# One third of nine table loads is split into DMAs of 16, 35, 35, 21 and 21 rows

## The chip, the core and the metric

The kernel runs on one core of a Trainium2 chip. A core has five engines that run their own instruction streams: PE (TensorE, matrix products), DVE (VectorE), ACT (ScalarE), POOL (GpSimd) and SP (SyncE, here used only to issue DMAs). Sixteen DMA engines move data between HBM, the chip's large memory, and SBUF, the core's 128-partition working memory. PSUM is the small memory that PE writes into. The metric is the device time of one launch in microseconds (us); the median of ten runs is compared.

## The reference

For each of 1024 users the function gathers up to 50 item embeddings of length 128, forms running means over time, normalizes them over the batch, feeds them through a leaky integrate-and-fire step, and multiplies the mean spike count with the whole embedding table.

```python
emb = emb_table.at[0].set(0.0)              # 100001 x 128, float32
e = emb[seq]                                # seq: 1024 x 50
prefix = jnp.cumsum(e, axis=1)
denom = jnp.minimum(t_idx[None, :], lengths[:, None]).astype(e.dtype)
uF = prefix / denom[:, :, None]
y = (uF - uF.mean(axis=0)) * lax.rsqrt(uF.var(axis=0) + BN_EPS) * gamma + beta
def step(v, x):
    v = v + (x - v) / TAU
    spike = atan_spike(v - V_TH)            # 1 where v >= V_TH
    return (v - spike * V_TH, spike)
_, spikes = lax.scan(step, v0, moveaxis(y, 1, 0))
scores = spikes.mean(axis=0) @ emb.T        # 1024 x 100001, float32
```

The scores alone are 409.6 MB, and they must be written to HBM.

## The kernel before

**First stage.** The loop `for t in range(T)` gathers the 50 time steps with indirect DMAs on POOL, accumulates them in PSUM, and does the statistics and the spike step on DVE and ACT. It ends with the spike counts in `countA`, `countB` and `countC`, 128 users to a block of columns.

**Second stage.** The table is cut into 98 parts of 1024 rows (`HALF`); the last has 673. `WIDTHS` groups the parts into 21 column groups of the output: 4 of two parts, 4 of three, then 13 of six (the last a little narrower). For each column group `c` and each of the 8 blocks of users `n`, PE multiplies the counts with the split table parts (`product`, line 154 of the file), DVE and ACT take turns in copying the sums out of PSUM into an output tile `o` (lines 483 and 485), and SP stores that tile with one DMA (`store`, line 163). From the ninth group on such a store is 128 rows of 24 KB, 3 MB in all, and there are three output tiles in turn, so that the filling of one tile waits until the store of three before has landed.

**The loads.** A part of the table lies in SBUF as 128 partitions with 8 rows of 512 bytes each, 4 KB in one piece. `fetch(r, q, n)` loads `n` parts starting with part `q` into the row tile `r`. The first 38 parts (`held`) are loaded by SP during the first stage. The others are loaded by ACT in the second stage, three parts at a time (`GROUP // 2`), after the second and the fifth block of a column group (`n in (1, 4)`), so that there are two loads to a column group; two row tiles take turns. Such a load is one DMA of 1.5 MB (line 102) with 384 pieces of 4 KB. Later `prepare` transposes a part on PE, and ACT and DVE split it into a high and a low half.

```python
            if n in (1, 4) and c >= MIDDLE and to_fetch < parts:
                g, k = divmod(to_fetch - TWICE, GROUP)
                if k or to_split >= (g - 1) * GROUP + TWICE:
                    ...
                    fetch(r, to_fetch, GROUP // 2)
                    to_fetch += GROUP // 2
```

The last load is shorter: two whole parts (line 102), then the tail part in a DMA of five times 128 rows (line 111) and one of 33 rows (line 116).

**Order.** The kernel records its instructions in program order for each engine (`manual_schedule`). SP and ACT are in-order: a DMA that must wait holds up everything behind it on the same engine. Completion of the DMAs of SP and ACT is told by eight semaphores, used in turn (the trace names them 101 to 106, 117 and 118); a DMA is issued only when the one that had the same semaphore eight DMAs earlier has landed.

Of the kernel before, what the change touches and what calls it, by code (L numbers as in the profile page):

```python
# [20 lines left out]
P = 128  # L21
BN_EPS = 1e-5
V_TH = 1.0
HALF = 1024
KQ = HALF // P
BANK = 512
GROUP = 6
# [3 lines left out]

WIDTHS = 4 * [2] + 4 * [3] + 13 * [6]
NARROW, MIDDLE = 4, 8


@with_exitstack
def rec_kernel(
# [38 lines left out]
    held = AHEAD * GROUP + TWICE  # L76
# [8 lines left out]
    def size(q):  # L85
        return min(HALF, N - q * HALF)

    def group(g):
        at = g if g < AHEAD else AHEAD - 2 + g % 2
        r = rowp.tile([P, GROUP, HALF], F32, tag=f"rows{at}", name=f"rows_{g}")  # L90
        for k in range(GROUP):
            rows[g * GROUP + (TWICE if g else 0) + k] = r[:, k, :]
        return r

    def fetch(r, q, n):

        engine = nc.sync if q < held else nc.scalar
        k = q if q < GROUP else (q - TWICE) % GROUP
        n = min(n, parts - q)
        whole = n - (size(q + n - 1) < HALF)  # L100
        if whole:
            engine.dma_start(
                out=r[:, k : k + whole, :],
                in_=table[q * HALF : (q + whole) * HALF, :].rearrange("(q p k) d -> p q (k d)", p=P, k=KQ),
            )
        if whole < n:
            full, rest = divmod(size(parts - 1), P)
            c1 = (parts - 1) * HALF
            r = r[:, k + whole, :].rearrange("p (k d) -> p k d", d=D)
            if full:  # L110
                engine.dma_start(
                    out=r[:, :full, :],
                    in_=table[c1 : c1 + full * P, :].rearrange("(k p) d -> p k d", p=P),
                )
            if rest:
                engine.dma_start(out=r[:rest, full, :], in_=table[c1 + full * P : N, :])
# [49 lines left out]
    with ExitStack() as ph:  # L166
# [16 lines left out]
        nc.sync.dma_start(out=gb[:, 1:2], in_=beta.rearrange("(d o) -> d o", o=1))  # L183
        first = group(0)
        fetch(first, 0, GROUP)
        for g in range(1, AHEAD):
            fetch(group(g), g * GROUP + TWICE, GROUP)
# [91 lines left out]
        def over(t, v):  # L279

            d = lp.tile([P, B], BF16, tag="d", name=f"d_{t}")
            nc.scalar.activation(d, v, AF.Identity, bias=less)  # L282
            return d
# [7 lines left out]
        whole = slice(0, B)  # L291
# [6 lines left out]
        for t in range(T):  # L298
# [33 lines left out]
            r = sp.tile([P, 1], F32, tag="r", name=f"r_{t}")  # L332
# [14 lines left out]
            q = sp.tile([P, 1], F32, tag="q", name=f"q_{t}")  # L347
# [20 lines left out]
            if not last:  # L368
# [6 lines left out]
                d = over(t, v)  # L375
# [3 lines left out]
                if t in (T - 8, T - 6):  # L379
                    q = (t - T + 8) // 2  # L380
                    pair(q)
                    prepare(q, vp.tile([P, HALF], F32, tag="v1", name=f"pt_{q}"))
                    if q == TWICE - 1:
                        for k in range(TWICE):
                            rows[GROUP + k] = first[:, k, :]
                        nc.sync.dma_start(
                            out=first[:, :TWICE, :],
                            in_=table[GROUP * HALF : (GROUP + TWICE) * HALF, :].rearrange(
                                "(q p k) d -> p q (k d)", p=P, k=KQ
                            ),  # L390
# [48 lines left out]
    for c, W in enumerate(WIDTHS):  # L439
# [30 lines left out]
        for n in range(NB):  # L470
# [26 lines left out]
# [3 lines that stand above are left out]
                    if k == 0:  # L500
                        r = group(g)
                    fetch(r, to_fetch, GROUP // 2)
                    to_fetch += GROUP // 2
# [21 lines left out]
```

## Time and profile before

| What | Value |
|---|---|
| Median of 10 runs | 1579.63 us (1578.96 to 1580.17) |
| The profiled execution's own time | 1579.85 us |
| Its span, first to last instruction | 1577.7 us |
| Mean granted clock of TensorE | 0.941 |
| Bytes from HBM, to HBM | 77.69 MB, 409.60 MB |
| Busy share of the span: PE, DVE, ACT, POOL | 72%, 60%, 42%, 25% |
| First load of the second stage is issued | 782.2 us |
| Last load of the second stage is issued | 1416.6 us |

The span leaves out some 2.2 us around the instructions (1579.85 less 1577.7). The busy shares are means over two stages with different limits: the first stage ends at about 520 us and hardly uses the DMA engines after its start, the second uses them all the time.

### The profile page before, as it was taken

How to read it: one execution, taken by the hardware profiler on the slowest of the kernel's cores; microseconds unless marked ns; L12 is line 12 of the kernel's file. 1: busy time of each engine (PE TensorE's matmuls, PEld its weight loads, DVE VectorE, ACT ScalarE, POOL GpSimd, SP SyncE). 2: the span in 40 equal slices, each digit the busy share in tenths (PEclk: the TensorE clock that was granted, in tenths of full speed). 3: DMA queues.
4: the chain of work that ended last, by engine and by line, in shares of the span. 5: the costliest groups of instructions: out<-in, count | busy, mean ns of one | idle time of the engine just before them, and what ended most of it. 6: DMA issues, size and time to landing. Idle time of an engine off the chain costs nothing.

```text
span 1577.7 us, 12239 instructions
## 1 busy us (share of the span) xinstructions
PE 1128.8 (72%) x4450; PEld 801.4 (51%) x4450; DVE 945.0 (60%) x1125; ACT 668.2 (42%) x697; POOL 387.9 (25%) x408
## 2 busy tenths in 40 slices
PE   4544444444445988889887888888888787888884
PEld 2211111111122766668666666666666676666663
DVE  5777777767777665567555545545555545545552
ACT  2333333333333554555444444444444444444542
POOL 7777777777777000000000000000000000000000
PEclk9999999999975999999999999999999989999997
DMA  9611111111121899999999999999999999999998
GB/s 350 233 52 53 52 54 52 52 53 52 53 79 47 345 416 403 422 419 402 421 431 429 430 428 427 417 422 428 417 414 417 423 428 423 414 416 425 406 429 340
DMA packets 51897, 488.12 MB, mean 309 GB/s; under 512 B 10075, under 2 KB 11004, under 8 KB 30588
## 3 DMA queue, kind: packets, MB, share of 16 engines
q1 hardware_dynamic: 30464, 429.81, 64.8%
q0 software_dynamic: 12800, 26.24, 5.7%
q10 hardware_dynamic: 8572, 31.28, 5.0%
q8 instruction: 35, 0.57, 0.1%
q14 instruction: 26, 0.21, 0.0%
HBM read 77.69 MB, written 409.60 MB: 309 GB/s over the span
## 4 chain that ended last, share of the span: by engine, by line
DMA 52%; POOL 18%; PE 12%; issue 8%; ACT 5%; DVE 2%; another core or an unknown queue 0%; ACTq 0%; SPq 0%; POOLq 0%; DVEq 0%
DMA scores<-o 45%; POOL e L196 18%; PE po L154 11%; DMA e<-in_L_rec_emb_table,idx 5%; ACT o L485 5%; DMA rows<-in_L_rec_emb_table 2%; DVE o L483 1%; PE pt L124 0%; ACT pairs L146 0%; PE pre L309 0%; DVE pairs L147 0%; DMA idx<-in_r_seq 0%; DVE uF L318 0%; ACTq L485 0%
## 5 line engine op out<-in xcount | busy, mean ns | idle before, releaser
L483 DVE TENSOR_SCALAR o<-po 128x1024 f32<-128x1024 f32 x391 | 464.4, 1221 | 345.6 <-DMA scores<-o 304.2
L485 ACT ACTIVATE o<-po 128x1024 f32<-128x1024 f32 (+1 forms) x391 | 389.2, 1018 | 541.5 <-DMA scores<-o 319.8
L196 POOL DMA_INDIRECT e<-in_L_rec_emb_table,idx x400 | 382.3, 956 | 123.7 <-issue 112.4
L154 PE MATMUL po<-pairs,countB 128*128 128x512 f32 x1136 | 303.5, 413 | 63.3 <-ACT o L485 46.4
L309 PE MATMUL pre<-ident,e 128*128 128x128 f32 x400 | 180.8, 464 | 231.7 <-DMA e<-in_L_rec_emb_table,idx 231.3
L154 PEld LDWEIGHTS po<-pairs,countB 128*128 128x128 f32 x1136 | 217.6, 197 | 125.5 <-ACT o L485 61.1
L154 PE MATMUL po<-pairs,countC 128*128 128x512 f32 x852 | 236.4, 424 | 50.5 <-ACT o L485 50.4
L309 PEld LDWEIGHTS pre<-ident,e 128*128 128x128 f32 x400 | 73.3, 184 | 342.0 <-DMA e<-in_L_rec_emb_table,idx 341.2
L154 PEld LDWEIGHTS po<-pairs,countC 128*128 128x128 f32 x852 | 166.8, 202 | 96.5 <-ACT o L485 62.1
L147 DVE TENSOR_TENSOR pairs<-pt,pairs 128x1024 fp32r<-128x1024 f32 x71 | 86.2, 1222 | 95.6 <-ACT pairs L146 95.4
L318 DVE SCALAR_TENSOR_TENSOR uF<-rlen,pre 128x512 f32<-128x512 f32 x100 | 68.3, 683 | 112.7 <-PE pre L309 112.6
L124 PE MATMUL pt<-ident,rows 128*128 128x128 f32 x782 | 112.9, 292 | 9.0 <-issue 4.9
L124 PEld LDWEIGHTS pt<-ident,rows 128*128 128x128 f32 x782 | 102.1, 153 | 27.4 <-issue 12.9
L333 ACT ACTIVATE r<-mv,eps 128x1 f32<-128x1 f32 x50 | 14.8, 295 | 226.4 <-DVE mv L329 226.4
L154 PE MATMUL po<-hi,countB 128*128 128x512 f32 x216 | 88.2, 408 | 17.6 <-ACT o L485 12.7
L270 PE MATMUL pre<-zT,ls 128*128 128x512 f32 x100 | 77.5, 777 | 23.0 <-DVE uF L318 19.1
L154 PE MATMUL po<-lo,countB 128*128 128x512 f32 x216 | 85.4, 397 | 0.0
L282 ACT ACTIVATE d<-v,less 128x1024 bf16<-128x1024 f32 x49 | 54.5, 1113 | 63.5 <-DVE v L366 63.5
L154 PE MATMUL po<-hi,countC 128*128 128x512 f32 (+1 forms) x162 | 68.8, 425 | 14.7 <-ACT o L485 14.7
L146 ACT CAST pairs<-pt 128x1024 fp32r<-128x1024 f32 x71 | 71.8, 1012 | 15.3 <-PE pt L124 15.1
L154 PE MATMUL po<-pairs,countA 128*128 128x512 f32 x284 | 71.0, 394 | 6.7 <-ACT o L485 6.7
L363 ACT ACTIVATE v<-uF,hgb,a 128x1024 f32<-128x1024 f32 x49 | 59.2, 1208 | 30.5 <-DVE a L359 30.5
(78 smaller groups left out, 824.6 us busy)
## 6 DMA issues: line engine op xcount, KB each, us to landing
scores<-o SPq DMA_DIRECT2D x96, 3072.0 KB, 20.2
scores<-o SPq DMA_DIRECT2D x32, 1536.0 KB, 8.9
scores<-o SPq DMA_DIRECT2D x30, 1024.0 KB, 8.6
rows<-in_L_rec_emb_table ACTq DMA_DIRECT2D x19, 1536.0 KB, 29.1
scores<-o SPq DMA_DIRECT2D x8, 2896.5 KB, 17.3
rows<-in_L_rec_emb_table SPq DMA_DIRECT2D x6, 3072.0 KB, 27.8
e<-in_L_rec_emb_table,idx POOLq DMA_INDIRECT x400, 2.5
rows<-in_L_rec_emb_table SPq DMA_DIRECT2D x1, 1024.0 KB, 4.8
```

Source lines behind the costliest of these rows:

```text
L124: nc.tensor.transpose(pt[:, k0 : k0 + kw], r[:kw, k0 : k0 + D], ident[:kw, :kw])
L146: nc.scalar.copy(vh, vp)
L147: nc.vector.tensor_tensor(vl, vp, vh.bitcast(F32), ALU.subtract)
L154: nc.tensor.matmul(po[:, :kw], lhsT=counts[n], rhs=part[:, k0 : k0 + kw], start=j == 0, stop=j == 1,)
L196: nc.gpsimd.indirect_dma_start(out=es[t][:, n * P : (n + 1) * P], out_offset=None, in_=table, in_offset=bass.IndirectOffsetOnAxis(ap=idx[: ...
L270: nc.tensor.matmul(pre[h], lhsT=l, rhs=zT[:, h * BANK : (h + 1) * BANK], start=t == 0, stop=False, skip_group_check=True,)
L282: nc.scalar.activation(d, v, AF.Identity, bias=less)
L309: nc.tensor.matmul(pre[h][:, k : k + P], lhsT=e[:, h * BANK + k : h * BANK + k + P], rhs=ident, start=False, stop=last, is_transpose=True, ...
L318: nc.vector.scalar_tensor_tensor(uF[:, cs], rlen[:, cs], 1.0 / (t + 1), pre[h], ALU.max, ALU.mult)
L363: nc.scalar.activation(vt, uF[:, cs], AF.Identity, bias=hgb[:, 1:2], scale=a)
L483: nc.vector.tensor_scalar_mul(o[:, h0 : h0 + hw], po[:, :hw], 1.0 / T)
L485: nc.scalar.mul(o[:, h0 : h0 + hw], po[:, :hw], 1.0 / T)
```

## The change

In `fetch`, every second load of the second stage, starting with the first, nine in all, takes its third part out of the one large DMA. The third part's 128 partitions are loaded by five DMAs of 16, 35, 35, 21 and 21 partitions, issued by ACT in front of the DMA that now has two parts. The bytes and their places in SBUF stay the same.

```diff
+FEWER = range(0, 18, 2)
+PIECES = (16, 35, 35, 21, 21)
...
         n = min(n, parts - q)
         whole = n - (size(q + n - 1) < HALF)
+        if (q - held) // (GROUP // 2) in FEWER:
+            whole -= 1
+            n = whole
+            one = r[:, k + whole, :]
+            src = table[(q + whole) * HALF : (q + whole + 1) * HALF, :].rearrange("(p k) d -> p (k d)", k=KQ)
+            p0 = 0
+            for pw in PIECES:
+                engine.dma_start(out=one[p0 : p0 + pw, :], in_=src[p0 : p0 + pw, :])
+                p0 += pw
+            assert p0 == P
         if whole:
             engine.dma_start(
                 out=r[:, k : k + whole, :],
```

## The prediction

> **What bounds the kernel now.** I read the page's slices first (DMA share and GB/s), then its chain.
>
> ```profile
> DMA  9611111111121899999999999999999999999998
> GB/s 350 233 52 53 52 54 52 52 53 52 53 79 47 345 416 403 422 419 402 421 431 429 430 428 427 417 422 428 417 414 417 423 428 423 414 416 425 406 429 340
> ...
> DMA 52%; POOL 18%; PE 12%; issue 8%; ACT 5%; DVE 2%; another core or an unknown queue 0%; ACTq 0%; SPq 0%; POOLq 0%; DVEq 0%
> ```
>
> From the fourteenth slice on the DMA engines are full at 400 to 430 GB/s, and half of the chain is DMA. The change touches only this second stage, so I cut it by stage: the load period, then the pure stores.
>
> ```profile
> core 0: us, PE busy (x) PEld busy (x) DVE busy (x) ACT busy (x) POOL busy (x), PEclk, DMA share, GB/s
> ...
> 782.00:1437.00 655.00, 540.01 (x2337) 425.33 (x2335) 342.76 (x291) 287.72 (x292) 0.00 (x0) 0.93 1.00 423
> 1437.00:1570.00 133.00, 101.92 (x446) 80.01 (x446) 68.84 (x61) 54.25 (x58) 0.00 (x0) 0.94 0.98 417
> ```
>
> A DMA share of 1.00 beside PE 82% busy: transfers set the pace. The DMA view of 782 to 1577 us gives their prices.
>
> ```profile
> q1 hardware_dynamic: 13863, 301.12, 89.1%
> q10 hardware_dynamic: 8572, 31.28, 9.9%
> ...
> scores<-o SPq DMA_DIRECT2D x87, 3072.0 KB, 20.3
> rows<-in_L_rec_emb_table ACTq DMA_DIRECT2D x19, 1536.0 KB, 29.1
> ```
>
> q1 holds the stores, q10 the loads. A store puts 8 packets of 24 KB on each of 16 engines; a load puts 24 packets of 4 KB on each. The packet records show an engine taking one of each in turn, 0.912 us and 0.159 us at best, which makes a load take 29.1 us.
>
> The mean hides what matters here. The trace keeps 16 landing times for each DMA, one an engine. For the last store they are 1569.7 to 1569.9 (eight), 1570.3 to 1570.5 (four), 1571.5 to 1571.7 (three), and one alone at 1576.7. From about 860 us on nearly every store has such a laggard, 4 to 8 us behind. Followed packet by packet from 975 us, it is one engine: 0.93 us a 24 KB packet against 0.92 for the others, and never idle. The other fifteen are idle 76 engine-us between 782 and 1562 us, 5.1 us each. **So one DMA engine sets the end, and the other fifteen have 5.1 us of idle and 5.0 to 7.0 us at the end to spare: 10.1 to 12.1 us.**
>
> **What moves.** A DMA of 128 partitions leaves 16 completion packets, that of 33 (line 116) leaves 11, with three rows each where I could follow it: the largest number up to 16 that divides the rows. By that 16 rows go to sixteen engines, 35 and 21 to seven. For a split load each of the seven then carries 1+5+5+3+3+16 = 33 packets in place of 24, each of the nine others 1+16 = 17. A 4 KB packet costs 9.9% of 16 x 795 us over 31.28 MB, that is 0.165 us (0.159 at best; 0.162 taken). Over nine loads:
>
> - each of the seven: 9 x 9 x 0.162 = 13.1 us more;
> - each of the nine: 9 x 7 x 0.162 = 10.2 us less.
>
> The completion packets (9 ns) add 0.2 us at most. PE, DVE and POOL keep their instructions in the same order.
>
> Is the laggard among the seven? It is one of the 11 that served the 33-row DMA: its sequence shows three 512-byte packets after its share of line 111. No row says more; counting places alone would give 7 in 11. I take it to be outside, as a judgment, and keep 8 in 100 for the other case. The Trainium skill ("DMA: Bandwidth & Descriptors", "Why a DMA increments its semaphore by 16 and not by 1") says that a DMA from SP or ACT uses the lowest-numbered k engines, and under "Latency and other measured facts" that engines 7 and 15 are usually slower. By that page the laggard, within the lowest eleven, would be engine 7, just outside the lowest seven; no run here shows the numbers.
>
> **The sum.** The laggard ends 10.2 us earlier and stops being last. The seven take up 13.1 us with 10.1 to 12.1 to spare: 1.0 to 3.0 us late. If none of the 5.1 us of idle can be filled, 8.0. The idle sits in three places (about 1165, 1365 and 1465 us), after fast engines ran dry behind the laggard; engines with more work have a longer queue, so I take most of it as filled: 3.0 + 1.0 = 4.0 us. The profiled 1579.85 becomes 1583.85; the median of the runs is 0.22 lower, so 1583.6. Own range: 1580 to 1588.
>
> **Issue on ACT.** Five more DMAs a load, 45 in all.
>
> ```profile
> 782.23 0.42 ACTq L102 DMA_DIRECT2D rows<-in_L_rec_emb_table  x1
> 786.68 1.94 ACT L485 ACTIVATE o<-po 128x1024 f32<-128x1024 f32 x2 [3.43 <-DMA scores<-o]
> ...
> 1416.64 1.74 ACTq L116 DMA_DIRECT2D rows<-in_L_rec_emb_table  x1
> ```
>
> The nearest rows are 0.37 us (the median of line 102) and 1.74 us (line 116, 33 rows): 1.9 to 8.7 us a load. After an issue ACT waits some 4.0 us anyway (782.65 to 786.68), for a store's landing. So 0 to 4.7 us of lateness for the next evictions; behind them stand stores that take 20.3 us to land where 8 packets need 7.3, some 13 us of queue. I enter 0; with that queue gone it would be up to 9 x 4.7 = 42 us, which a DMA share of 1.00 excludes. The skill's "Rules for kernel authors" on the same page advise against this change: merge small transfers, under 64 KB is mostly overhead. By its fixed 2.0 us a DMA an estimate would be 45 x 2.0 = 90 us more if nothing overlapped. The rows here show overlap: loads of 29.1 us run beside stores at 423 GB/s.
>
> **The added waits.** Eight completion semaphores are used in turn; a split load takes six. In the changed build a column group's first store waits for the landing of the second load of the group before, which did not bind earlier. That load, issued at 875.8, landed at 904.9 and the store was issued at 905.5. Behind nine more packets, each in turn with a store's, it lands up to 9 x (0.912 + 0.159) = 9.6 us later, and SP waits as long, with only further stores queued behind. Such a wait exists already:
>
> ```profile
> SPq L163 <- DVE o L483: 647.4, 92, 11.2
> SPq L163 <- ACT o L485: 72.4, 84, 1.5
> SPq L163 <- DMA rows<-in_L_rec_emb_table: 26.2, 3, 12.5
> ```
>
> Three such waits of 26.2 us in total left the laggard without idle time, since its queue was full. The seven will be in its place, so I enter 0. ACT's second load waits for the second piece, six packets (6.4 us) after an issue 26 us earlier: free. The rows of a part are needed a column group (some 67 us) later: free.
>
> **The rivals.**
>
> - *Faster (20%).* If the idle belonged to the seven alone, each would have 76/7 = 10.9 us and with 7.0 at the end 17.9 us to spare: 13.1 fits, and the end comes 4.8 us earlier, 1575.0. It decides from 16.3 us to spare on. For it: three of the fifteen end 1.8 us later and show less idle. Against: nothing ties the others' idle to the seven. A 24 KB packet takes 0.925 us on the mean against 0.912; less crowding could give part of that, so the low end is 1574.
> - *No shift (10%).* The rows go evenly over the sixteen, or the shift just balances: within 2 us of 1579.6. Against it stand the 11 completion packets.
> - *The laggard is one of the seven (8%).* It never idles, so all 13.1 us show: 1593.
> - *The new wait drains the seven (7%).* Landing, SP's issue and the first packet are about 0.45 + 0.35 + 1.2 = 2.0 us without work in each of nine column groups, 18 us on top of 4: about 1602. It decides where the seven have less than two store packets left when the second load lands. Against: 13 us of queue.
>
> **Chances.** The main case has 55%. About 0.2%, 3.2 us, is what a measurement of this kernel can tell from no change. Of the main case's range of 1.0 to 8.0 about a third lies below that: 18% within, 37% slower. With the rivals: slower 37 + 8 + 7 = 52%, same 18 + 10 = 28%, faster 20%. The range runs from the faster rival's low end, 1574, to the laggard among the seven, 1593, and leaves out the drained queue and some tails.
>
> **What would show it.** Right: stores from about 1000 us on land on nine engines first and on seven several us later; the split loads' two-part DMA lands 35 us after its issue; the laggard no longer stands alone; in the windows the load period grows from 655 us by some 4 us. Wrong: one landing alone stays last (the laggard is among the seven if it is later than 7 us, or nothing moved if as before); the DMA share of 782 to 1437 falls below 0.97 with SP's waits for rows above 60 us (drained queue); or the seven land level with the nine by the end (more room than I counted).

## The result, and the profile after

| | before | after |
|---|---|---|
| Median | 1579.39 us (28 runs) | 1591.44 us (8 runs) |
| Span of the profiled execution | 1577.7 us | 1589.9 us |
| Ratio | | 1.0077, 95% interval 1.0068 to 1.0085 |

The change costs 12.05 us. The forecast was 1583.6 us (+4.0); the range reached up to 1593 for one rival, "the laggard is one of the seven". The profile was read in the same order as before: slices and chain of the page, then by stage.

```profile
DMA  9611111111121999999999999999999999999998
GB/s 348 231 52 53 51 53 53 51 54 53 51 80 41 384 416 405 423 414 406 426 423 417 428 407 394 423 410 428 394 419 423 401 424 407 425 418 421 407 421 341
...
DMA 56%; POOL 19%; PE 9%; issue 8%; ACT 4%; DVE 2%; another core or an unknown queue 0%; ACTq 0%; SPq 0%; POOLq 0%; DVEq 0%
```

The DMA engines are as full as before in tenths, but the rate dips below 410 GB/s in more slices, and DMA has a larger part of the chain (56% against 52%). By stage (core 0: PE, PEld, DVE, ACT and POOL busy with counts, the granted clock, the DMA share, GB/s):

```profile
782.00:1437.00 655.00, 540.06 (x2294) 419.02 (x2293) 338.21 (x286) 281.28 (x287) 0.00 (x0) 0.92 0.99 416
1437.00:1583.00 146.00, 111.12 (x494) 87.23 (x492) 74.00 (x65) 59.59 (x63) 0.00 (x0) 0.94 0.98 415
```

In the same 655 us the DMA engines moved 416 GB/s in place of 423, some 4.6 MB less, which is 11 us at 417 GB/s; PE had 2294 matmuls done instead of 2337. So the loss arises in the load period, and the pure stores after it run as before.

The DMA view from 782 to 1590 us: the queues (packets, MB, share of 16 engines), then issues with their number and size.

```profile
q1 hardware_dynamic: 13863, 301.12, 87.7%
q10 hardware_dynamic: 8968, 31.28, 9.6%
...
rows<-in_L_rec_emb_table ACTq DMA_DIRECT2D x10, 1536.0 KB
rows<-in_L_rec_emb_table ACTq DMA_DIRECT2D x10, 1024.0 KB
rows<-in_L_rec_emb_table ACTq DMA_DIRECT2D x18, 140.0 KB
rows<-in_L_rec_emb_table ACTq DMA_DIRECT2D x18, 84.0 KB
```

The loads' bytes are the same, and their packets took 9.6% of 808 us where they took 9.9% of 795, about the same time: the transfers themselves did not become dearer.

The waits of SP's queue from 782 to 1590 us (us in total, times, the longest):

```profile
SPq L175 <- DVE o L495: 503.6, 72, 11.1
SPq L175 <- DMA rows<-in_L_rec_emb_table: 132.3, 14, 13.3
SPq L175 <- ACT o L497: 64.7, 67, 2.8
SPq L175 <- DMA scores<-o: 57.8, 9, 10.3
```

Here the waits for `rows` rose from 26.2 to 132.3 us and waits for earlier stores are new. This looks like the forecast's drained queue ("SP's waits for rows above 60 us"); its other sign, a DMA share below 0.97, is absent. Which is cause and which effect cannot be read here, so this wait became a rival for the runs.

The landing times tell more. Those of the last store, and in the middle of the load period those of a DMA of 35 rows and of the two-part DMA of the same load (us, each in order):

```
last store            1581.7 1581.7 1581.7 1581.8 1581.8 1581.8 1581.9 1581.9 1581.9 1581.9 1581.9 1581.9 1583.5 1583.7 1583.7 1588.7
35 rows, at 1060.7    1066.5 1067.5 1067.5 1067.7 1067.7 1067.9 1076.6
two parts, at 1063.3  1084.0 1084.1 1084.1 1084.2 1084.2 1084.2 1084.2 1084.3 1084.3 1090.8 1091.8 1091.8 1092.0 1092.1 1092.2 1100.5
```

The third row shows the shift: nine engines, then six, then one. The second has seven landings, and one of them is 8.7 us behind the other six. The first still has one landing alone, 5.0 us after the next. Followed back packet by packet, the engine of that last landing is without work for 1.2 us in all between 790 and 1553 us. The trace gives a packet's times and not its engine; but a packet mostly begins 3 to 4 ns before the end of the one ahead of it on its engine, and a store puts eight on each engine, so the packets can be sorted by engine, apart from single ones. With those of 785 to 1200 us sorted in this way, the late engine has a part in every one of the 24 DMAs of 35 and 21 rows, and takes 0.934 us a 24 KB packet where the other fifteen take 0.920 to 0.927. So the late engine is one of the seven. Whether its added packets are the whole cost, or the many DMAs have a part in it, this trace cannot tell; the runs below were made for that.

### The profile page after: what moved, and what is told of

Its sections match the earlier page's. It is cut to its first block, busy times and chain, and to the rows that moved or that the text cites. A ratio compares the mean times of both kernels' runs of the same rounds, so it can differ in the third digit from the quotient of the medians.

```text
span 1589.9 us, 12311 instructions
## 1 busy us (share of the span) xinstructions
PE 1138.0 (72%) x4450; PEld 801.6 (50%) x4450; DVE 945.1 (59%) x1125; ACT 667.1 (42%) x697; POOL 388.0 (24%) x408
## 4 chain that ended last, share of the span: by engine, by line
DMA 56%; POOL 19%; PE 9%; issue 8%; ACT 4%; DVE 2%; another core or an unknown queue 0%; ACTq 0%; SPq 0%; POOLq 0%; DVEq 0%
DMA scores<-o 46%; POOL e L208 19%; PE po L166 9%; DMA e<-in_L_rec_emb_table,idx 5%; DMA rows<-in_L_rec_emb_table 4%; ACT o L497 4%; DVE o L495 1%; ACT pairs L158 0%; PE pt L136 0%; DVE pairs L159 0%; DMA idx<-in_r_seq 0%; PE pre L321 0%; DVE uF L330 0%; DVE centred L348 0%
## 5 line engine op out<-in xcount | busy, mean ns | idle before, releaser
L166 PE MATMUL po<-pairs,countB 128*128 128x512 f32 x1136 | 309.8, 419 | 64.3 <-ACT o L497 58.9
L166 PEld LDWEIGHTS po<-pairs,countB 128*128 128x128 f32 x1136 | 220.9, 200 | 131.0 <-ACT o L497 73.3
L136 PE MATMUL pt<-ident,rows 128*128 128x128 f32 x782 | 109.2, 286 | 10.6 <-issue 4.9
L136 PEld LDWEIGHTS pt<-ident,rows 128*128 128x128 f32 x782 | 97.4, 149 | 30.3 <-issue 11.3
```

Of the source, the lines that this page charges most:

```text
L136: nc.tensor.transpose(pt[:, k0 : k0 + kw], r[:kw, k0 : k0 + D], ident[:kw, :kw])
L166: nc.tensor.matmul(po[:, :kw], lhsT=counts[n], rhs=part[:, k0 : k0 + kw], start=j == 0, stop=j == 1,)
```

## The experiments

**Theories.** A: one DMA engine is late already before the change, it is one of the seven, and its nine more packets a load are the whole cost. B: the 45 extra DMAs cost it, through ACT's time for issuing them or through the waits that they bring to SP. The price for A is the change's own: 12.05 us for 9 x 9 = 81 packets, 0.149 us each.

**1. The same number of DMAs, evenly over the engines.**

```diff
-PIECES = (16, 35, 35, 21, 21)
+PIECES = (16, 32, 32, 32, 16)
```

> The same nine loads in the same five extra DMAs, but of 16, 32, 32, 32 and 16 rows, so that each DMA divides by 16 and every engine carries 24 load packets as before. Theory A (the late engine is one of the seven and pays for nine more packets a load): nothing is added to it, 1579.4 us within 1.5, ratio 1.000 to 1.001. Theory B (the 45 extra DMAs cost it, by some 1.2 us of ACT's time each or by the waits that they bring to SP): as slow as the change, 1588 to 1592 us, with SP's waits for rows near 130 us. If both work, the time lies between.

Measured: 1580.4 us against 1579.92, ratio 1.0003 (0.9994 to 1.0012). The extra DMAs are all there and cost at most 0.12%, 1.9 us. The waits of SP's queue from 782 to 1577 us:

```profile
SPq L175 <- DVE o L495: 557.5, 83, 11.2
SPq L175 <- DMA scores<-o: 91.3, 9, 10.4
SPq L175 <- ACT o L497: 71.2, 75, 2.3
SPq L175 <- DMA rows<-in_L_rec_emb_table: 26.0, 3, 12.5
```

The waits for `rows` are back at 26.0 us, and nine waits for `scores`, 91.3 us, have come from the turn of the eight semaphores; they are as many as in the changed kernel, and cost nothing that can be measured. The 132.3 us after the change are thus an effect of the loads' late landing. B falls.

**2. The same shift with fewer DMAs.**

```diff
-PIECES = (16, 35, 35, 21, 21)
+PIECES = (119, 9)
```

> The same shift with 18 extra DMAs in place of 45: 119 rows (17 on each of seven engines) and 9 rows (one on each of nine). By the rule of the largest divisor each of the seven then carries 34 load packets a split load, two of the others 17, seven 16. Theory A: 90 packets more on the late engine where the change had 81; at the change's 12.05 / 81 = 0.149 us each 13.4 us, so 1592.8 us (1591.5 to 1594). Theory B: 18/45 of 12 us, 1584 us (1582 to 1586).

Measured: 1592.23 us against 1579.92, ratio 1.0079 (1.0065 to 1.0093). It is the packets on the lowest engines that are paid, not the DMAs: 18 extra DMAs cost 12.3 us as 45 did. By stage:

```profile
782.00:1437.00 655.00, 535.86 (x2286) 419.93 (x2286) 337.53 (x286) 282.04 (x286) 0.00 (x0) 0.92 0.99 415
```

The load period shows what it shows after the change: 415 GB/s and PE some 50 matmuls behind.

**3. A ladder of small DMAs.**

```diff
-PIECES = (16, 35, 35, 21, 21)
+PIECES = [(112, j, 16 - j) for j in range(1, 10)]
...
-            for pw in PIECES:
+            for pw in PIECES[(q - held) // GROUP]:
```

> In the nine split loads, in order, the third part comes in DMAs of 112, j and 16 - j rows with j = 1 to 9: one row on each of j and of 16 - j engines. Every landing time is kept. If engines are taken from a fixed end of the row of sixteen, the landing that is 4 to 8 us later than the rest is missing in the DMAs of few rows and present from some count on, the same in both halves of the ladder; for theory A that count is 7 or lower. If the late landing appears only in DMAs of 8 rows and more, theory A is wrong. If it comes and goes without order, the engines are not taken from a fixed end. The time is within 2 us of before if the late engine is in about half of them.

Measured: 1581.94 us, one run. This was inconclusive, by a fault of its design: a DMA of j and one of 16 - j rows both take the same end of the row of engines, so the ladder itself loaded the first engines more and more (nine packets more on the first, nine fewer on the last), and from about 1190 us on six landings were late together.

**4. The same ladder without weight.** The steps are now 64 bytes wide; the edit is to the kernel before.

```diff
+FEWER = range(0, 18, 2)
+PROBE = (7, 7, 7, 1, 2, 3, 4, 5, 6)
...
+            j = PROBE[(q - held) // GROUP]
+            for p0, p1, d0, d1 in ((0, 112, 0, HALF), (112, P, 16, HALF), (112, 112 + j, 0, 16), (112 + j, P, 0, 16)):
+                engine.dma_start(out=one[p0:p1, d0:d1], in_=src[p0:p1, d0:d1])
```

> A probe that shifts no load: of the third part, 112 rows whole and 16 rows without their first 16 elements go to sixteen engines, and the 64 bytes left in each of the 16 rows come in two DMAs of j and 16 - j rows. From the fourth split load on (985 us, from where one engine was seen to be late before) j is 1, 2, 3, 4, 5, 6; before it 7. If a DMA of j rows uses the same j engines each time, the late landing is in the DMA of j rows from some j on, and in that of 16 - j rows always as long as the two share the engine. Theory A: it is in those of 7 rows, and the j from which on it is seen, less one, is its place in the row of sixteen. If it is at place 0, it is in all of them. Time: as before, 1578.5 to 1581 us.

Measured: 1580.79 us, one run. The landings of the DMAs of j rows (us, in order):

```
j = 1   994.3
j = 2  1061.8 1061.9
j = 3  1128.1 1128.3 1128.5
j = 4  1196.0 1196.1 1196.9 1196.9
j = 5  1264.0 1264.1 1264.1 1264.2 1269.5
j = 6  1331.4 1331.5 1331.6 1332.2 1332.3 1337.3
```

Up to four rows nothing is late; from the fifth row on exactly one landing is, by 5 us. (In the DMAs of sixteen landings of the same loads four or five engines lag, so this alone would leave open which of them is last at the end.) A second reading settles that: the engine of the last landing of all, followed back to 790 us, took 2, 2, 2, 1, 1, 1, 1, 2, 2 of the 64-byte packets in the nine loads. The engine at the fifth place must have that row: two where both DMAs reach it (j = 7, 5, 6), one where only the longer does (j = 1 to 4); no other place has it. So a DMA of k rows uses the same first k engines each time, and the late engine is the fifth. The Trainium skill ("DMA: Bandwidth & Descriptors", "Why a DMA increments its semaphore by 16 and not by 1") says the same of the DMAs of SP and ACT: they take the lowest-numbered k engines.

**5. The forecast's main case made true: the shift without the fifth engine.**

```diff
-FEWER = range(0, 18, 2)
-PIECES = (16, 35, 35, 21, 21)
+FEWER = (0, 2, 6, 8, 12, 14)
+PIECES = (68, 60)
```

> The forecast's main case made true: the probe has put the late engine at the fifth place, so a shift onto the first four leaves it out. In six of the loads the third part comes as 68 rows (17 on each of four engines) and 60 rows (four on each of fifteen): each of the four carries 37 load packets in place of 24, the late engine 20. Six loads: 78 packets more on each of the four, 12.6 us at 0.162 (the change: 81 on seven). If the forecast's sum holds, with 10.1 to 12.1 us to spare and most of the idle filled, they end 0.5 to 3.5 us late: 1580.4 to 1583.4 us. If only the 5.0 to 7.0 us at the end are to spare, 1585.5 to 1587.5. If there is nothing to spare and the late engine's place does not matter, 1592.

Measured: 1577.23 us against 1579.65, ratio 0.9985 (0.9976 to 0.9994): faster, by 2.4 us. The dose on the loaded engines is nearly that of the change (12.6 us against 13.1). The last store lands at 1571.4 to 1571.7 (eleven), then 1572.1, 1573.2, 1573.3, 1573.4 and 1574.1: nobody is alone any more. By stage, 782 to 1437 and 1437 to 1570 us:

```profile
782.00:1437.00 655.00, 530.17 (x2340) 416.58 (x2339) 344.39 (x292) 287.96 (x293) 0.00 (x0) 0.95 1.00 422
1437.00:1570.00 133.00, 99.90 (x444) 77.96 (x442) 66.85 (x60) 52.78 (x56) 0.00 (x0) 0.95 0.98 415
```

The rate is nearly that of before, 422 GB/s against 423, beside a shift as large on each loaded engine as that of the change. What matters is that the fifth engine is now outside. Sorted by engine, the packets up to 1300 us show four that take part in every DMA of 68 rows, and an engine outside the four that takes 0.934 us a 24 KB packet, where the other fifteen take 0.913 to 0.923. The waits of SP's queue in the same run:

```profile
SPq L175 <- DVE o L495: 598.2, 86, 11.2
SPq L175 <- DMA rows<-in_L_rec_emb_table: 80.8, 8, 15.9
```

A kernel that is faster than before waits 80.8 us for rows where before waited 26.2: this wait is no cost by itself, as the new waits for `scores` were none in run 1.

**6. The same in nine loads.** (`FEWER` as in the change, `PIECES = (68, 60)`.)

> The same in all nine loads: 117 packets more on each of four engines, 19.0 us, and 36 fewer on the late engine. With 10.1 to 12.1 us to spare 6.9 to 8.9 us late, 1586.8 to 1588.8 us; with 5.0 to 7.0 to spare 1592 to 1594; with nothing 1599. The four should then land last, level with each other, and the late engine before them.

Measured: 1583.36 us against 1579.65, ratio 1.0023 (1.0014 to 1.0032), 3.7 us slower; below everything that was expected. Here the four are loaded past their room. Sorted by engine, the packets of 980 to 1414 us show the four with 0 to 0.9 us of idle each, and the other twelve, the late one among them, with 8.7 to 17.4 us. That the four land last, as expected, the last store's landings do not show (eleven at 1579.7 to 1579.9, then 1580.6, 1581.6, 1581.7, 1581.7, 1582.5): they do not name their engines. If the four set the end, they had 19.0 - 3.7 = 15.3 us to spare by the forecast's 0.162 us a packet, or 117 x 0.149 - 3.7 = 13.7 us by the price that the late engine showed. The forecast had counted 10.1 to 12.1, and had half of the idle as lost.

**7. The same in three loads.**

```diff
+FEWER = range(0, 18, 6)
+PIECES = (68, 60)
```

> The same in three loads only: 39 packets more on each of four engines, 6.3 us, which the spare takes if it is 6 us or more, and 12 fewer on the late engine, 12 x 0.149 = 1.8 us. The theory (the fifth engine sets the end) expects 1578.1 us against 1579.9, ratio 0.9989 (0.9982 to 0.9995), which is at the edge of what five rounds can tell; with 5.0 us to spare 1.3 us slower; with nothing to spare 1586.

Measured: 1577.93 us against 1579.65, ratio 0.9988 (0.9979 to 0.9997): -1.7 us where -1.8 was worked out from 12 packets fewer. One landing is still alone last, 3.1 us after the next (1574.8 against 1571.7). Followed back, the engine of that landing is again outside the four and takes 0.934 to 0.939 us a 24 KB packet in every 100 us up to 1414 us. Within the interval, its packets have the same price downwards as upwards.

**8. Other addresses for the same engine.**

```diff
-    outs = out.rearrange("(p n) c -> n p c", n=NB)
+    outs = out.rearrange("(n p) c -> n p c", n=NB)
```

The two loads of the user data follow (`(n p) t -> p n t`, `(n p) -> p n`).

> The kernel before with users in another order: partition p and block n hold user 128 n + p in place of 8 p + n, so the rows that one engine writes stand side by side in HBM and at other addresses; the computation is the same. If the fifth engine itself is slow, one landing is again last alone, 4 to 8 us behind, at 0.93 us a 24 KB packet. If the addresses that it wrote were slow, the landings close up or several engines share the lag, and the time falls by up to 5 us.

Measured: 1580.64 us, one run. One landing stays last alone throughout, 4.0 us after the next for a store at 1273.9 us (1294.2 against 1290.2), 2.0 us at the end; sorted by engine from 945 to 1414 us, its engine is the only one that never idles. It took 0.934 us a 24 KB packet, twelve others 0.920 to 0.925 and three others 0.936 to 0.938, with 1.8 to 2.1 us of idle each. So the lag does not hang on the addresses in HBM, and the time of a packet in one stretch does not single the engine out. That it is again the fifth engine was not sought in this run, and whether the engine or the part of SBUF that it reads is slow was not tried.

**9. Five engines in place of four.** The same six loads:

```diff
-PIECES = (68, 60)
+PIECES = (95, 33)
```

> The contrast of four and five engines, in the same six loads: 95 rows (19 on each of five engines) and 33 rows (three on each of eleven), where the run with four engines had 68 and 60. The first five then carry 38 load packets in place of 24, the others 19 or 16. As many extra DMAs, and nearly the same weight on the engines that are loaded; what differs is that the fifth engine is now among them: 84 packets more on it. The theory expects 84 x 0.149 = 12.5 us over before, 1592 us (1590.5 to 1593.5). If it is not the fifth engine that sets the end, the time is within 2 us of the run with four, 1576 to 1580.

Measured: 1592.19 us against 1579.67, ratio 1.0078 (1.0064 to 1.0092); 12.5 us slower, as worked out. With 12 extra DMAs in six loads, and one engine more in the set, the time goes from 2.4 us under before to 12.5 us over it. By stage, and the waits of SP's queue:

```profile
782.00:1437.00 655.00, 535.73 (x2290) 419.89 (x2290) 338.57 (x286) 281.48 (x286) 0.00 (x0) 0.92 0.98 415
```

```profile
SPq L175 <- DMA rows<-in_L_rec_emb_table: 67.4, 6, 14.7
```

The rate in the load period is nearly that of the changed kernel, 415 GB/s against 416, while SP waits for rows only half as long as there: again that wait does not carry the cost. The last store has one landing alone, 1589.3 after 1584.4.

**10. Four engines in five loads, for the best dose.**

```diff
+FEWER = range(0, 18, 4)
+PIECES = (68, 60)
```

> 68 and 60 rows in five of the loads, every second of the nine. The late engine carries 20 packets fewer, 20 x 0.149 = 3.0 us, and the first four 65 more, 10.5 us, less than the 13.7 to 15.3 us that the run in nine loads showed them to have. Expected 1576.7 us (1575.5 to 1578), ratio 0.998; if the five loads run into the others' own limit as six did, 1577.3.

Measured: 1577.58 us against 1579.67, ratio 0.9987 (0.9978 to 0.9996). The last landing is 2.2 us behind the next, where six loads left 0.7. Three, five and six loads cannot be told apart by these runs; all three are faster than the kernel before, by about 2 us. This run also settles a point of place: the record lists chip 6 for runs 1 to 4, chip 2 for runs 5 to 8 and chip 13 for runs 9 and 10. The probe found the fifth place on chip 6, and the contrast of four and five engines stands on chip 13 alone (runs 10 and 9).

## Why the prediction was right in its range and wrong in its likeliest case

- **One DMA engine sets the end.** Right. It did before, it does after, and taking 12 packets off it gave 1.7 us back. "It is one engine: 0.93 us a 24 KB packet against 0.92 for the others" holds for the mean of the others only. In the kernel before it is alone up to 900 us (0.935 against 0.913 to 0.918 for each of the others). Between 945 and 1300 us three others are as slow (0.938), and what sets it apart is that it alone has no idle; these three are likely the three landings 1.8 us behind the first.
- **Sixteen, seven and nine: the rule of the largest divisor.** Right: the first split load's two-part DMA, issued at 789.0 us, lands on nine engines after 21.4 to 23.4 us and on seven after 35.6 to 36.9 (35 was expected), and the runs with 119, 68 and 95 rows behaved by the same rule.
- **The judgment that the laggard lies outside the seven. This is the step that failed.** Nothing in the profile said so; the 33-row DMA put it among eleven, by which counting places gave 7 in 11 for inside. The forecast put it at 8 in 100, as a judgment, beside the page's sentence that engines 7 and 15 are usually slower, under "Latency and other measured facts". The same row gives a cause, as a guess, that it ties to the DMAs of POOL; the loads and stores of this stage come from ACT and SP. Here the measurement decides: counted from 0 the late engine is number 4. With the 7 in 11 that the rows gave, the likeliest time would have been 1593.
- **13.1 us more on each of the seven.** Right in kind, and near in size: 12.05 us. That is 0.149 us a packet where 0.162 was taken; the run with 90 packets gives 12.3 / 90 = 0.137, the one with 84 0.149. The late engine hardly idles before or after, so the missing tenth is not idle time of its own; where it comes from was not found.
- **10.1 to 12.1 us to spare on the others.** Too small: 13.7 to 15.3 by run 6, if the four set its end. And "if none of the idle can be filled, 8.0" (13.1 less the 5.0 at the end is 8.1), with most of it entered as filled, was too careful: with the fifth engine left out, a shift of 12.6 us made the kernel 2.4 us faster, where the same sum gives 0.5 to 3.5 us slower. So the main case had a second error, in the other direction; with the right side guessed it would still have forecast a loss where there is a gain. The "faster" rival, with 17.9 us to spare, was the nearer one for such a shift. The room is not fixed: in run 5 the four loaded engines have 0 to 1.9 us of idle between 786 and 1300 us, while the eleven that are neither loaded nor late have 8.5 to 11.5 us. A likely reason, not tried by itself: an engine idles because the latest one holds the output tiles.
- **Issue on ACT at 0.** Right, within 1.9 us for 45 DMAs. But the 4.0 us that ACT waits anyway were used up. The end of such an issue in the timeline of ACT after the change:

```profile
1061.92 1.34 ACTq L110 DMA_DIRECT2D rows<-in_L_rec_emb_table  x2
1063.29 0.62 ACTq L114 DMA_DIRECT2D rows<-in_L_rec_emb_table  x1
1064.09 2.86 ACT L497 ACTIVATE o<-po 128x1024 f32<-128x1024 f32 x3 [4.00 <-PE po L166]
```

  The column behind the start is busy time. This load's six issues run from 1059.07 to 1063.91 us, so the 4.00 us of idle before the next eviction are spent in issuing; it begins 0.18 us after the last issue, with three evictions in a row where ACT had two after the load at 782.2 us before. The lateness was covered by the stores in the queue. The median of the 45 issues at line 110 is 1.20 us, between the forecast's bounds of 0.37 and 1.74. "45 x 2.0 = 90 us more if nothing overlapped", worked out from the page's fixed cost of about 2 us a DMA, which stands there for DMAs of POOL, did not come: the even pieces, with as many DMAs, cost at most 1.9 us.
- **The added waits at 0.** Right in price, although they came: 91.3 us of new waits in the run with even pieces, for nothing. "SP's waits for rows above 60 us" was a poor sign of a drained queue, because loads that land late lengthen it as well.
- **The signs.** "One landing alone stays last (the laggard among the seven if it is later than 7 us)" named the right view with a wrong bound: it is 5.0 us later than the next. The bound took the others' end as fixed, and they too end 12 us later (1581.7 against 1569.7). "The load period grows by some 4 us" and "the laggard no longer stands alone" came out wrong, both for the same failed step.
- **The sign.** Slower was the side with most of the chance, 52%, but the path to it was the one that had been given 8 in 100. That the range of 1574 to 1593 held is due to this rival alone; the main case's own range, 1580 to 1588, was missed. The right sign was luck.

## What to carry to other kernels

When a transfer-bound stage ends with one landing alone, find out which engine that is before moving rows: small DMAs of one to sixteen rows and 64 bytes told its place here in one run, together with its packets followed back from the last landing. A DMA whose row count has no divisor near 16 used only the first few engines here (35 rows seven, 68 four, 95 five); if the late one is among them, all that is added to it is paid (12 us for 81 packets of 4 KB), and if it isn't, the same DMA relieves it (2.4 us gained). A wait that grows fivefold in the profile (26.2 to 132.3 us) may be the effect: undo the suspected cause alone, here the DMAs' number, before pricing it.

## What the runs showed of the hardware

- One DMA engine out of sixteen is a little slower throughout, 0.93 to 0.94 us a 24 KB packet, with other addresses too, where most others take 0.91 to 0.93. That is enough to set the end of a stage of 790 us. The probe puts it at the fifth place, and the runs with four, five and seven engines, on three chips, agree.
- A DMA that uses k engines with k below 16 leaves k landings and one further update of its semaphore about 1.5 us after issue, long before any data has landed (for the DMA of 35 rows issued at 1060.67 us it came at 1062.1 us, the first landing at 1066.5).
- On ACT an issue right behind another is the dear one, with pieces on seven engines and with pieces on sixteen alike. The first piece of the load at 1059 us took 0.335 us and the two of 35 rows behind it 1.20 and 1.22. The median of the 45 pieces is 1.20 us after the change, and 1.23 with the even pieces, which use all sixteen engines; a whole load alone took 0.37 us before.
